# Where step 1 counts its put-off rows on TensorE: at the end of an iteration, pinned in program order

## The chip, the cores and the metric

The kernel runs on one core of one Trainium2 chip. The metric is the device time of one execution in microseconds (us), lower is better; a time is the median of several executions. Engines are named as in the profile: PE is TensorE's matmul side and PEld its weight loads, DVE is VectorE, ACT is ScalarE, POOL is GpSimd, SP is SyncE, which here only issues DMAs.

## What is computed

Four graph layers over 4096 nodes with 256 features, each followed by a residual and a layer norm. Layers 0, 2 and 3 are products of a 0/1 adjacency matrix with the features. Layer 1 is the one that matters here; it runs two steps (n = 0 and n = 1) of

```
logits = q @ k.T                 # 4096 x 4096, q and k from the current Xa
probs  = softmax(logits)
A      = for each row, keep the largest probs until their sum reaches 0.9, renormalize
Xf     = R @ Xf                  # R: the adjacency matrix + I, its rows scaled to sum 1
Xa     = A @ Xa
Z      = Z + Xf @ U1[n].T + Xa @ U2[n].T
```

The kernel never sorts a row of 4096. It finds the threshold of each row from the largest values of 18 groups of columns (step 1), and a row for which that is not sure is put off: it is marked bad, its number goes into a list in HBM, and the listed rows are computed later, 128 at a time, by a slower way that always works.

## The kernel before, in words

Rows are worked on in tiles of 128. In step 1, `run_step(1, ...)` (L944) has an iteration for each tile i from -2 to 31, in which three tiles are in flight:

- tile i+2 (`nxt`): its logits are made, in eight chunks of 512 columns (g = 0 to 7, NLC = 8), by PE (`logits_chunk`, L415) and copied out by ACT (L416).
- tile i+1 (`cd`): DVE takes the group maxima (`peak_groups`, L434, 18 instructions, and L466, L467), ACT the exponentials (L457), DVE the largest 72 candidates (`tops`, L529 and L533), the threshold and the mark bad (`pick`, L551 to L566). Then `flag` (L584) counts the bad rows, and `settle` (L643) zeroes what lies under the threshold: one pass over the row for ties (L660) and four passes over quarters of it (L665).
- tile i (`st`): PE transposes its kept probabilities (`turn`, L746, copied out by ACT, L749) and multiplies them with Xa (L769). One iteration later `mix` (L816) turns the result (L186, ACT L188), multiplies it with U1 and U2 (L822), and DVE adds the residual (L824) and does two layer norms, each with one power on POOL (L200).

From tile 11 on, an iteration also makes one row tile of the product with R (`neighbours`: ACT L685, PE L688, ending in L690). Three times (after i = 9, 20 and during i = 31) 128 put-off rows are taken from the list (`take_rows`, L883) and become a job, whose stages (`put_off`, L897; five probes of L499, then candidates and settling) run beside the ordinary tiles.

`pieces` (L725) writes the iteration as a loop over g; after the work of chunk g it runs the functions that `run_step` has put down for g with `at(g, f)`. So `at(4, flag, cd)` (L1018) traces the flag after the logits, the product and the neighbours of chunk 4.

What `flag` issues for a tile: two matmuls of one column, L594 (sum of `bad` over the tile, on all partitions) and L595 (bad rows before each row), into one half of the PSUM bank `mm_bank`; three small DVE instructions that turn them into places in the list (`sofar` L597, `slot` L601, `slots` L602); and one indirect DMA from POOL that writes the row numbers into `list_d` (L608). `query` (L395) and `mix` (L822) use the same bank. `take_rows` loads 128 entries of the list (L888, on SP's queue), clamps them (`from_l`, L890, DVE) and gathers their rows (L812, POOL).

The order in which each engine gets its instructions is not the traced order. The framework plans it: it simulates the engines with durations of its own, and gives an engine, among the instructions whose inputs are ready in that simulation, the one traced first. On the chip each engine then follows this fixed order, and an instruction whose input is late holds up all that stand behind it on its engine. `tc.keep_in_program_order(ins)` adds an edge of order (no semaphore, no instruction) from the instruction traced just before on the same engine to `ins`: the planner may place `ins` only behind that one. It doesn't keep later traced instructions from being placed ahead of `ins`.

Of the kernel before, what the change touches and what calls it, by code (L numbers as in the profile page):

```python
# [57 lines left out]
def gnn_stack(ctx, tc, x, adjt, adjn, w0, b0, w1, w2t, w3t, u1t, u2t, ln_g, ln_b, w2, b2, w3, b3, out):  # L58
# [3 lines left out]
    nc = tc.nc  # L62
# [3 lines left out]
    NLC = N // LC  # L66
# [20 lines left out]
    def half(bank):  # L87
        turns[bank] ^= 1
        return (mm_bank if bank == "mm" else acc_bank)[:, turns[bank], :]
# [90 lines left out]
    def transposed(*srcs):  # L180

        n = 2 * len(srcs)
        ps = ps_tr.tile([P, 4, P], F32, tag="tr", name="tr")
        for s, src in enumerate(srcs):
            for c in range(2):
                nc.tensor.transpose(ps[:, 2 * s + c, :], src[:, c * P : (c + 1) * P], ident)  # L186
        t = work.tile([P, 4, P], F32, tag="xt", name="xt")
        nc.scalar.copy(t[:, :n, :], ps[:, :n, :])  # L188
        return t
# [168 lines left out]
    with tc.tile_pool(name="l1", bufs=1, reuse_waits="tile") as l1:  # L358

        cur = {"late": False, "n": 0, "nef_done": False}  # L360
# [4 lines left out]
        ones_sq = l1.tile([P, P], F32, name="ones_sq")  # L365
# [23 lines left out]
        def query(xi, xt=None):  # L389

            if xt is None:
                xt = transposed(xi)
            ps = half("mm")
            for c in range(2):
                nc.tensor.matmul(ps[:, :P], wq_sb[:, c, :], xt[:, c, :], start=(c == 0), stop=(c == 1))  # L395
            up = upper(ps[:, :P])
            q = [work.tile([P, P], F32R, tag=f"q{k}", name=f"q{k}", bufs=3) for k in range(2)]
            nc.scalar.copy(q[0], up)
            nc.vector.tensor_sub(q[1], ps[:, :P], up)
            return q  # L400
# [17 lines left out]
        def logits_in(l):  # L418

            nc.vector.memset(l[:, N:], -1.0)  # L420
            return l

        def small(tag, w=1, dt=F32, bufs=2):
            if cur["late"]:
                return cur["lw"].tile([P, w], dt, tag=tag, name=f"{tag}_l", bufs=2 if w == 1 else 1)
            return work.tile([P, w], dt, tag=tag, name=tag, bufs=bufs)
# [157 lines left out]
        def flag(st):  # L584


            pb = half("mm")
            later = st.get("later")
            if later is None:
                nc.tensor.matmul(pb[:1, 0:1], st["bad"], ones_col, start=True, stop=True)  # L590
                st["nb"] = small("nbad", 1, I32)[:1, :]
                nc.scalar.copy(st["nb"], pb[:1, :1])
                return
            nc.tensor.matmul(pb[:, 0:1], ones_sq, st["bad"], start=True, stop=True)  # L594
            nc.tensor.matmul(pb[:, 1:2], before, st["bad"], start=True, stop=True)  # L595
            sofar, slot = small("sofar"), small("slot")
            nc.vector.tensor_add(sofar, later["base"], pb[:, 0:1])  # L597

            i = st["tile"]
            at, rows_i = slots_of[cur["n"]][:, i : i + 1], ids[:, i : i + 1]  # L600
            nc.vector.scalar_tensor_tensor(slot, pb[:, 1:2], later["base"], spare, op0=ALU.add, op1=ALU.subtract)  # L601
            nc.vector.scalar_tensor_tensor(at, slot, st["bad"], spare, op0=ALU.mult, op1=ALU.add)  # L602
            later["base"] = sofar
            if i == NT - 1 and cur["n"] == 0:

                st["to"] = to = small("to_last", 1, I32, 1)
                nc.vector.scalar_tensor_tensor(to, st["bad"], float(P), rows_i, op0=ALU.mult, op1=ALU.add)
            nc.gpsimd.indirect_dma_start(  # L608
                out=list_d[cur["n"]], out_offset=bass.IndirectOffsetOnAxis(ap=at, axis=0), in_=rows_i, in_offset=None)
# [314 lines left out]
        def left_over(n, e, later):  # L924

            count = work.tile([P, 1], I32, tag="count_l", name="count_l", bufs=1)
            nc.vector.tensor_scalar(count, later["base"], float(P - 1 - LATER[n] * P), 0.0, op0=ALU.add, op1=ALU.max)
            nc.vector.tensor_scalar(count, count, P.bit_length() - 1, None, op0=ALU.arith_shift_right)
            v = nc.values_load(count[0:1, 0:1], min_val=0, max_val=NT - LATER[n])
            with tc.For_i(0, v, 1) as k:  # L930
                cur["late"] = True
                st, xg = take_rows(n, bass.ds(k * P + LATER[n] * P, P), e)
                all_logits(st, query(xg))
                peak(st)
                exp_rows(st)
                st["t"], st["left"], st["base"] = small("t_thr"), small("left"), None
                for _ in settle(st, True):
                    pass
                pieces(n, st, None, {})
                for f in after(n, st):  # L940
                    f()
                cur["late"] = False

        def run_step(n, es):  # L944
# [37 lines left out]
            for i in range(-2, NT):  # L982
                st = tiles.pop(i, None)
                cd = tiles.get(i + 1)
                nxt = None
                if i + 2 < NT:

                    nxt = {"tile": i + 2, "q": cur["qs"].pop(0), "e": logits_in(es[i % 2]), "later": later, "G": {}}
                    tiles[i + 2] = nxt
                if i + 1 == NT and n == 0:  # L990
                    for fs in last:
                        for f in fs:
                            f()
                    last = []
                    left_over(n, es[NT % 2], later)
                ops = {}

                def at(g, f, *args):
                    ops.setdefault(g, []).append(lambda: f(*args))

                for g, fs in zip((1, 2), last):
                    for f in fs:
                        at(g, f)
                if 0 < i + 2 < NT - 1:
                    turned = []
                    g = 1 if n else 6
                    at(g - 1, lambda i, turned: turned.append(transposed(cur["xa"][:, i + 3, :])), i, turned)
                    at(g, lambda turned: cur["qs"].append(query(None, turned[0])), turned)
                if cd is not None:
                    peak_groups(cd, NG_LATER if n else ngr)  # L1010
                    at(1, exp_rows, cd)
                for job in jobs:
                    at(1, advance, job)
                if cd is not None:
                    rounds = ROUNDS if n else ROUNDS_FEW
                    at(2, tops, cd, rounds)
                    at(2, pick, cd, rounds)
                    at(4, flag, cd)  # L1018
                    if n == 0:
                        for k in range(8):  # L1020
                            at(4 + k // 2, gather, cd, k)
                    else:
                        at(5, lambda cd: [None for _ in settle(cd)], cd)
                if n == 0 and st is not None:
                    for k in range(8, KEPT):
                        at(k // 2 - 4, gather, st, k)
                for job in jobs:
                    if n and i + 1 == NT:
                        at(4, advance, job)
                    at(6, advance, job)  # L1030
                if i + 1 == NT and n == 0:
                    cur["next"] = load_halves(es[1 - NT % 2], xf_d, nc.sync)
                if i < 0:
                    now = FIRST[n][i + 2]
                else:
                    now = [i + 2] if FIRST[n][1][-1] < i + 2 < NT else []
                pieces(n, st, nxt, ops, now)
                last = [[f] for f in after(n, st)] if st is not None else []
                if i in starts:
                    k = starts[i]  # L1040
                    if len(jobs) > (i == NT - 2):
                        last = finish(jobs.pop(0), last)
                    e = es[NT % 2] if k + 1 == LATER[n] else es[2]
                    jobs.append({"stages": put_off(n, k, e, later)})
                    if i < NT - 2:
                        advance(jobs[-1])
# [185 lines left out]
```

## Time and profile before

| what | us |
|---|---|
| median of 3 runs (3055.0 to 3058.85) | 3057.41 |
| the profiled execution | 3159.93 |
| its span, first to last instruction | 3158.2 |
| what lies around the span | 1.7 |
| mean granted TensorE clock | 0.971 |
| PE busy in the span | 2895.0 (92%) |
| DVE busy | 2247.3 (71%) |
| ACT busy | 1723.6 (55%) |
| POOL busy | 678.1 (21%) |
| first and last flag of step 1 on PE (from the span's start) | 1387.43 and 2439.92 |

The profiled execution is longer than the median of the other runs; all times of instructions are from it and are set against its own 3159.93 us. In a list of waits a line says which engine and line waited for which, then the sum in us, how often, and the longest. In a timeline the columns are the start in us from the span's start, the duration in us, and the instruction; x4 means four merged into one row, and a bracket at the end is the idle time of the engine just before it and what ended that.

### The profile page before, as it was taken

The page shows a single profiled execution, that of the slowest core. Times are in us where ns is not written, and L with a number is a line of the kernel's source. Part 1 is how long each engine was busy: PE and PEld are TensorE (multiplying, and loading weights), DVE is VectorE, ACT ScalarE, POOL GpSimd, SP SyncE. Part 2 cuts the span into 40 slices and gives each one's busy share as a digit, 9 for nine tenths or more (in the row PEclk, how much of TensorE's full clock was granted, in tenths as well). Part 3 has the DMA queues.
Part 4 walks back from the last instruction along what each step waited for, and adds up shares of the span by engine and source line. Part 5 has one row for each costly group of instructions (what it writes and reads, how often), then busy time and mean ns, then how long its engine had stood idle before and what let it go on. Part 6 is the DMA issues. An engine that isn't in the chain of part 4 may idle for free. (4 is left out here: it accounts for less than half of the span.)

```text
span 3158.2 us, 44761 instructions
## 1 busy us (share of the span) xinstructions
PE 2895.0 (92%) x14052; PEld 2271.4 (72%) x14052; DVE 2247.3 (71%) x7159; ACT 1723.6 (55%) x2883; POOL 678.1 (21%) x812
## 2 busy tenths in 40 slices
PE   7999888999999997789998999999999987999998
PEld 3788656777777775567777777878877645777886
DVE  4666667888888876267998999967999644444444
ACT  3555545566666654465554655546555425666664
POOL 1121245555555554000000000010000110000000
PEclk9999989999999998899999999999999998999999
DMA  9996455777777774240000111011110324333332
GB/s 172 158 178 126 77 100 110 122 131 132 128 130 136 132 133 132 79 110 17 26 23 26 30 35 38 29 36 32 34 38 24 104 92 158 108 108 95 107 109 77
DMA packets 242873, 286.82 MB, mean 91 GB/s; under 512 B 32928, under 2 KB 199776, under 8 KB 242624
## 3 DMA queue, kind: packets, MB, share of 16 engines
q0 software_dynamic: 41728, 91.69, 22.1%
q1 hardware_dynamic: 188656, 180.93, 18.6%
q10 hardware_dynamic: 12240, 11.23, 1.1%
q8 instruction: 114, 1.87, 0.2%
q14 instruction: 135, 1.11, 0.2%
HBM read 318.06 MB, written 66.32 MB: 122 GB/s over the span
## 5 line engine op out<-in xcount | busy, mean ns | idle before, releaser
L688 PE MATMUL acc_r<-xh,adjq 128*128 128x512 f32 x2048 | 625.9, 434 | 33.2 <-ACT adjq L685 17.5
L769 PE MATMUL acc_bank<-xa,at 128*128 128x256 f32 x2240 | 551.0, 386 | 26.2 <-ACT at L749 25.8
L685 ACT CAST adjq<-adj 128x512 fp32r<-128x512 fp8e4 x512 | 315.5, 619 | 371.0 <-PE acc_r L688 214.6
L688 PEld LDWEIGHTS acc_r<-xh,adjq 128*128 128x128 f32 x2048 | 382.8, 193 | 132.0 <-ACT adjq L685 37.7
L674 POOL DMA_INDIRECT G<-x_d,cols x416 | 403.5, 970 | 326.0 <-PE acc_bank L763 172.2
L769 PEld LDWEIGHTS acc_bank<-xa,at 128*128 128x128 f32 x2240 | 409.9, 193 | 85.9 <-ACT at L749 37.5
L416 ACT COPY e<-lg 128x512 f32<-128x512 f32 x544 | 315.1, 586 | 231.2 <-PE lg L415 159.9
L434 DVE MAX8 cand<-e 128x8 f32<-128x228 f32 (+1 forms) x1088 | 385.0, 399 | 34.4 <-ACT e L416 31.7
L415 PE MATMUL lg<-kS,q 128*128 128x512 f32 x1088 | 391.6, 442 | 6.0 <-issue 3.8
L200 POOL TENSOR_TENSOR rstd<-ve,mhalf 128x1 f32<-128x1 f32 x166 | 100.3, 604 | 1331.8 <-DVE ve L198 1246.3
L1112 ACT CAST a<-a 128x1024 fp32r<-128x1024 fp8e4 x256 | 268.3, 1049 | 165.4 <-PE acc L176 127.1
L531 DVE FIND_INDEX8 cols<-top,e 128x8 uint32<-128x4096 f32 x64 | 282.8, 4419 | 0.0
L176 PE MATMUL acc<-xh,a 128*128 128x512 f32 x1024 | 260.1, 407 | 21.2 <-DMA a<-adj_d 16.1
L176 PE MATMUL acc<-y0h,a 128*128 128x512 f32 x1024 | 249.9, 397 | 0.0
L176 PEld LDWEIGHTS acc<-xh,a 128*128 128x128 f32 x1024 | 191.7, 190 | 67.8 <-ACT xh L152 23.5
L176 PE MATMUL acc<-yh,a 128*128 128x512 f32 x1024 | 237.9, 394 | 0.0
L763 PE MATMUL acc_bank<-G,dg 128*128 128x256 f32 x832 | 228.1, 392 | 8.3 <-DVE dg L761 4.1
L176 PEld LDWEIGHTS acc<-yh,a 128*128 128x128 f32 x1024 | 192.2, 188 | 43.8
L176 PEld LDWEIGHTS acc<-y0h,a 128*128 128x128 f32 x1024 | 187.9, 188 | 39.0 <-issue 0.6
L749 ACT COPY at<-at_ps 128x512 f32<-128x512 f32 x288 | 168.7, 588 | 84.7 <-PE at_ps L746 83.0
L415 PEld LDWEIGHTS lg<-kS,q 128*128 128x128 f32 x1088 | 183.4, 193 | 29.6 <-ACT e L416 9.2
L763 PEld LDWEIGHTS acc_bank<-G,dg 128*128 128x128 f32 x832 | 156.3, 195 | 38.6 <-DVE dg L761 4.5
(287 smaller groups left out, 4414.1 us busy)
## 6 DMA issues: line engine op xcount, KB each, us to landing
adj<-adj_d SPq DMA_DIRECT2D x256, 128.0 KB
a<-adj_d SPq DMA_DIRECT2D x256, 128.0 KB
a<-in_adjt POOLq DMA_DIRECT2D x64, 256.0 KB
adj_d<-a SPq DMA_DIRECT2D x64, 256.0 KB
adjn<-in_adjn POOLq DMA_DIRECT2D x64, 256.0 KB
x_d<-x SPq DMA_DIRECT2D x64, 128.0 KB
xf_d<-xf_new SPq DMA_DIRECT2D x64, 128.0 KB
xf<-xf_d SPq DMA_DIRECT2D x64, 128.0 KB
```

What stands on the lines that cost most here:

```text
L176: nc.tensor.matmul(acc, a[:, j, :], halves(jt), start=(jt == 0), stop=(jt == NT - 1))
L415: nc.tensor.matmul(pl[:, :LC], q[k], kS[:, s], start=(k == 0), stop=(k == 1))
L416: nc.scalar.copy(l[:, s], pl[:, :LC])
L434: nc.vector.max(dst[:, 8 * g : 8 * g + 8], src[:, g * w : min((g + 1) * w, N)])
L531: nc.vector.max_index(st["at"][:, 8 * r : 8 * r + 8], t8, st["e"][:, :N])
L674: nc.gpsimd.indirect_dma_start(out=g, out_offset=None, in_=x1_d, in_offset=bass.IndirectOffsetOnAxis(ap=st["at"][:, k : k + 1], axis=0))
L685: nc.scalar.copy(a, cur["a8"][:, g % 2 * GP : (g % 2 + 1) * GP, :])
L688: nc.tensor.matmul(acc_r, a[:, j, :], xf[:, jt, :], start=(jt == 0), stop=False)
L749: nc.scalar.copy(at[:, :G, :], ps[:, :G, :])
L763: nc.tensor.matmul(acc_a, dg[:, k % 4, :], st["G"][k], start=(k == 0), stop=(k == KEPT - 1))
L769: nc.tensor.matmul(acc_a, ats[g][:, j, :], cur["xa"][:, jt, :], start=(jt == 0), stop=(jt == NT - 1))
L1112: nc.scalar.copy(a, a8)
```

## The change

In step 1 the flag is traced after the last chunk of the iteration (NLC - 1 is 7), and its first matmul is pinned behind what was traced before it on PE: the last matmul of the product (L769), or of the row tile of R (L690) where there is one. Step 0 keeps chunk 4 and gets no pin. Nothing is added to or taken from what the engines compute.

```
-            nc.tensor.matmul(pb[:, 0:1], ones_sq, st["bad"], start=True, stop=True)
+            total = nc.tensor.matmul(pb[:, 0:1], ones_sq, st["bad"], start=True, stop=True)
+            if cur["n"]:
+                tc.keep_in_program_order(total)
             nc.tensor.matmul(pb[:, 1:2], before, st["bad"], start=True, stop=True)
...
-                    at(4, flag, cd)
+                    at(NLC - 1 if n else 4, flag, cd)
```

## The prediction

> **What bounds the kernel now.** Only step 1's tiles are touched, 1387 to 2447 us, so I asked for the waits by stretch, not for the page's shares. First the sums of three stretches (length, then busy time of PE, PEld, DVE, ACT, POOL, the granted clock, DMA share, GB/s): 1445 to 1692 holds eight flags and no put-off job; the other two hold the jobs.
>
> ```profile
> 1445.00:1692.00 247.00, 228.29 (x1203) 191.60 (x1202) 226.23 (x780) 126.33 (x212) 18.70 (x25) 1.00 0.08 24
> 1735.00:2060.00 325.00, 309.83 (x1557) 254.95 (x1556) 300.22 (x1029) 184.86 (x306) 20.68 (x27) 0.99 0.13 33
> 2160.00:2440.00 280.00, 267.71 (x1357) 221.37 (x1355) 267.40 (x924) 153.81 (x258) 18.44 (x25) 1.00 0.14 33
> ```
>
> PE and DVE are both busy for 92 to 96%: each bounds the other, and a wait taken from one helps only as far as the other isn't late next. The waits of PE and then of DVE between 1735 and 2450 us:
>
> ```profile
> PE mm_bank L594 <- DVE bad L566: 15.8, 15, 1.7
> ...
> DVE h L824 <- PE mm_bank L822: 15.7, 9, 6.6
> ...
> DVE sofar L597 <- PE mm_bank L595: 4.2, 11, 1.8
> ```
>
> PE's largest wait is the flag's: 15.8 us at 15 of the 20 flags there, about 1.05 each. Between 1445 and 1692 the flag waits for nothing; PE waits are these:
>
> ```profile
> PE acc_bank L769 <- ACT at L749: 10.4, 8, 1.4
> PE mm_bank L395 <- DVE h L824: 8.3, 9, 1.0
> ```
>
> **Flags with a put-off job beside them.** PE's timeline at one of them, then DVE's:
>
> ```profile
> 1837.68 0.38 PE L594 MATMUL mm_bank<-bad,ones_sq 128*128 128x1 f32 x2 [1.32 <-DVE bad L566]
> ...
> 1841.66 3.75 PE L688 MATMUL acc_r<-xh,adjq 128*128 128x512 f32 x15
> 1845.26 1.03 PE L746 MATMUL at_ps<-ident,e 128*128 128x128 f32 x8
> ```
>
> ```profile
> 1843.60 1.27 DVE L665 SCALAR_TENSOR_TENSOR e<-e,t_thr 128x1024 f32<-128x1024 f32 x1
> ```
>
> The flag stops PE for 1.32 us. But the same tile's transposes (L746, 1845.26) need the first quarter of settle, done at 1843.60 + 1.27 = 1844.87: PE arrives 0.39 us after that. Without the flag's wait it would come 1.32 earlier and wait 0.93 there. So of each wait only the smaller of it and this slack comes back. For the 15 flags, in order: 0.16, 0.22, 0.38, 0.69, 0.32, 0.16, 0.26, 0.28, 0.41, 0.24, 0.41, 1.69, 0.26, 0.16, 1.19: 6.8 of 15.8 us; 9.0 move to L746. And an earlier PE shortens the run only where DVE waits for PE. In these iterations DVE's waits for h (L824) are 0.55, 6.61, 0.51, 0.33 and 3.25 us, and PE has 0.38, 0.69, 0.32, 0.41 and 0.26 to give them: 0.38 + 0.69 + 0.32 + 0.33 + 0.26 = 2.0. DVE's waits at sofar for the flag's matmuls go too, since the flag then stands where DVE finished bad long ago and reads it later: 4.2 less the one of 1.8 that lies outside the jobs, 2.4. Sum: **-4.4 us**.
>
> **Flags without a job** (nine, 1458 to 1693, 29.3 us apart). PE's timeline:
>
> ```profile
> 1632.40 1.89 PE L769 MATMUL acc_bank<-xa,at 128*128 128x256 f32 x8
> 1634.13 0.28 PE L594 MATMUL mm_bank<-bad,ones_sq 128*128 128x1 f32 x2
> 1634.27 0.36 PE L595 MATMUL mm_bank<-bad,before 128*128 128x1 f32 x2
> 1634.50 0.71 PE L415 MATMUL lg<-kS,q 128*128 128x512 f32 x2
> ...
> 1647.23 1.13 PE L769 MATMUL acc_bank<-xa,at 128*128 128x256 f32 x4 [1.12 <-ACT at L749]
> ```
>
> From the start of the eight L769 to the next L415 it is 2.10 us with the flag, 1.54 one chunk later without (1638.11 to 1639.65): a flag takes 0.56 us of PE. It lies between L395 and the last logits (1639.65), on the path: last logits, ACT copy, maxima, candidates, settle's tie pass (4.43), h, L395, logits again; PE's only idle time in it, 0.9 us, is at L395, ahead of the flag. At the end of the iteration (1642.03) the flag stands ahead of L746, L415 and L688, and behind those PE idles 1.1 to 1.4 us until ACT has done the exponentials: there it is free. That is 9 x 0.56 = 5.0. DVE can follow: it waits 0.57 us for the last logits, and POOL's list write (1.02 us, now just before the second L200 of a tile, where DVE waits 9.1/8 = 1.14 us against 9.9/21 = 0.47 with jobs) moves out of its way. The Trainium skill speaks against this sum: TensorE: Matmul & The Clock Gate, "Back-to-back issue gap", gives a matmul of 1 to 64 columns an issue floor of about 25 ns, so four (each of the pair runs as two) would be 0.1 us and the move worth 0.9 in all. The row has each with a weight load of its own (0.19) and 0.56 in sum; I take the row. **-5.0 us**, between 0 and -5.0.
>
> **The other flags**: 1387 and 1429 (the start) and 2041 to 2135 wait for nothing and PE is full there: 0.
>
> **What the move delays.** The three DVE instructions (0.13 + 0.21 + 0.22) only move. `mm_bank` is held from the flag until DVE has read it; next to want it is L822, 10.5 us after an iteration's end here (1642.2 to 1652.7), 12 in the row of 1837. A DVE instruction in the way lasts 4.4 at most, so 0; without that cover, up to 4.4 per tile. POOL: behind the list write wait L200 and the jobs' gathers; it takes 1.02 us and POOL is busy 7%: 0. SP: only the list's load waits for it, with the adjacency and row loads behind. The pin is an edge without a wait: 0.
>
> The list itself is needed at once three times. POOL's and SP's timelines at the first:
>
> ```profile
> 1694.36 1.02 POOL L608 DMA_INDIRECT list_d<-ids,slots  x1 [3.46 <-DVE kept L580]
> ```
>
> ```profile
> 1702.72 0.33 SPq L888 DMA_DIRECT2D to_l<-list_d  x1
> ```
>
> From the write's issue to the load 8.4 us pass, and then DVE stands still at L890: 5.58, 5.20 and 7.23 us (18.0 in sum). The Trainium skill's page DMA: Bandwidth & Descriptors ("Anatomy of one DMA — SWDGE (gpsimd) path") has a fixed cost of about 2.0 us for such a write: by it the list would be in HBM before DVE asks, and a later flag would cost nothing. The rows say 8.4, so each us of delay can be a us of DVE. The delays, from the flag to the last matmul that it is pinned behind: 1692.70 to 1700.6 = 7.9; 2074.71 to 2085.7 = 11.0; 2439.92 to 2446.4, of which DVE's tie pass (to 2444.5) and L205 already take all but 0.5. Bounds: if the planner moves L890 by as much, the wait stays as long and the price is 0.5; if L890 keeps its place, 7.9 + 11.0 + 0.5 = 19.4. I take 0.5, since L890 depends on the flag in the planner's simulation too; the 5 us of today are what that simulation has too little for a DMA, the same wherever it stands. The last job has cover besides: its settling ends its first quarter at 2552.5, and PE, at the zu matmuls (L871), comes to it at 2566.9.
>
> **Sum**: -4.4 - 5.0 + 0.5 = -8.9 us. The profiled execution would go from 3159.9 to 3151.0. The median of the runs shown is 3.2% lower; I take the difference over as it is: **3048.5**.
>
> **Rivals.**
> 1. Likeliest, as above: 3048.5, own range 3042 to 3055. Chance 0.45.
> 2. The wait only changes place. DVE is the bound with jobs, all 15.8 us come back at L746, and without jobs the planner fills the freed slot so that the flag's 0.56 is on the path again. For: the 9.0 us found above, DVE at 95%. Against: the idle time behind L688. 0, or 3057; that the planner lets later traced work pass the pinned flag, so that it stands in the next iteration and changes nothing, ends here too. Chance 0.22.
> 3. All of PE's wait is gain, since the planner moves L688 of R ahead of L746 and so hides the rest: -15.8 - 5.0 = 20.8, 3036.6. For: 15 L688 stand there in the row above. Against: DVE's idle time in these stretches is mostly not PE's doing. Chance 0.12.
> 4. Slower: the put-off rows come late. L890 stays where it is in DVE's order, and DVE, strictly in order, stands for 19.4 us more, with SP's loads behind L888: +19.4 - 8.9 = +10.5, 3067.9. It decides as soon as the list lands more than 8.9 us later, summed over the three loads, than L890's place in DVE's order moves. For: the 8.4 us of a list write, and DVE's 18.0 us there now. Against: the planner knows the dependence. Chance 0.21.
>
> Faster or slower by 0.2% is 6.1 us, about what a measurement of this kernel can tell from no change. Of rival 1, 0.35 lies beyond that and 0.10 within: faster 0.35 + 0.12 = 0.47, same 0.22 + 0.10 = 0.32, slower 0.21. The range reaches down to rival 3 and up to rival 4: 3037 to 3067.
>
> **What would show it.** Right: no wait of L594 for bad; L746 waits for L665, about 9 us in sum, in the iterations with a job; the nine iterations without one 28.7 us apart instead of 29.3, with the flag between L769 and L746 and less than 1.4 us idle at L769 behind L688; L205 there waiting about 0.5. L890 waiting 18 us in sum again. Wrong: L890 waiting over 27 us (rival 4), L822 or L395 waiting for slot (the bank), iterations still 29.3 us apart (rival 2), or a planner's order changed in more places than the flag's, which no step here prices.

## The result and the profile after

The changed kernel takes 3052.85 us (median of 19 runs, 3045.61 to 3062.08), the kernel before 3058.85 (19 runs beside it). The ratio is 0.9981, 95% interval 0.9973 to 0.9988: faster by 6.0 us, just short of the 6.1 us (0.2%) from which the prediction counts the kernel as faster. It had said 3048.5 and -8.9 us.

The profiled execution of the changed kernel takes 3051.51 us, that of before 3159.93. Nearly all of this difference lies in step 0, which the change doesn't touch: up to the first mark of step 1 (the end of DVE's L566 for tile 0) before needs 1374 us and the changed kernel 1275. The experiments show that this is no effect of the change: the kernel before needs 1272 us in another execution, and on one chip, where its median was 3157.66 us, every profiled kernel needs 1375 to 1377. So I compare from that mark on, with a second profiled execution of the kernel before (`before_again`, below). Lines of the changed kernel behind L596 have numbers that are higher by 2.

The same three stretches as before the change, the first two shifted by the 99 us, the third by 110:

```profile
1346.00:1593.00 247.00, 228.76 (x1209) 192.41 (x1208) 227.93 (x783) 127.36 (x214) 18.64 (x25) 1.00 0.09 24
1636.00:1961.00 325.00, 310.50 (x1568) 256.36 (x1568) 302.51 (x1043) 186.56 (x308) 21.17 (x28) 0.99 0.15 33
2050.00:2330.00 280.00, 268.66 (x1372) 223.90 (x1372) 269.54 (x935) 156.67 (x258) 18.47 (x25) 1.00 0.17 34
```

PE and DVE are busier by less than one per cent: DVE 227.93 us of 247 where it was 226.23. The waits of PE and DVE between 1636 and 2345 us say what became of the flag's wait:

```profile
PE at_ps L748 <- DVE e L667: 9.6, 10, 1.4
...
DVE h L826 <- PE mm_bank L824: 8.7, 5, 3.1
...
DVE m L466 <- DVEq L652: 4.2, 1, 4.2
...
PE mm_bank L594 <- DVE bad L566: 1.6, 2, 1.4
...
DVE sofar L599 <- PE mm_bank L597: 1.1, 4, 0.6
```

PE's wait at the flag falls from 15.8 to 1.6 us, and 9.6 of it stand at the transposes now, as forecast (9.0). DVE's wait for h falls from 15.7 to 8.7. Other waits of PE grow, for h at L395 from 1.4 to 5.5 us and for xt at L824 from 1.1 to 3.3, so that all of PE's waits in this stretch fall only from 32.1 to 28.5. The third line is new: DVE stands for 4.2 us at the register branch of a put-off job (L652).

At a flag without a job, PE's timeline is what the change meant it to be:

```profile
1483.70 0.81 PE L771 MATMUL acc_bank<-xa,at 128*128 128x256 f32 x3
1484.35 0.28 PE L594 MATMUL mm_bank<-bad,ones_sq 128*128 128x1 f32 x2
1484.49 0.36 PE L597 MATMUL mm_bank<-bad,before 128*128 128x1 f32 x2
1484.71 0.63 PE L748 MATMUL at_ps<-ident,e 128*128 128x128 f32 x4
...
1489.65 1.99 PE L771 MATMUL acc_bank<-xa,at 128*128 128x256 f32 x8 [1.07 <-ACT at L751]
```

Where the 6.0 us come from (us from mark to mark, the mark being the end of L566 of a tile; "end" is the end of the span):

| tiles | before_again | after | difference |
|---|---|---|---|
| 0 to 1 | 31.74 | 32.85 | +1.1 |
| 1 to 10, no job | 275.45 | 274.18 | -1.3 |
| 10 to 12, first list load | 81.89 | 81.45 | -0.4 |
| 12 to 20, first job | 273.20 | 273.33 | +0.1 |
| 20 to 23, second load | 133.17 | 128.69 | -4.5 |
| 23 to 31, second job | 266.98 | 262.93 | -4.1 |
| 31 to the end, third load | 718.25 | 721.26 | +3.0 |
| sum | 1780.7 | 1774.7 | -6.0 |

The first profile of before and `before_again` differ by up to 2.0 us in one such row. Set against the first profile the sum is -9.4, so it is luck that it is -6.0 here, as between the medians. The row beside the first job is the least steady: with the flags of tiles 11 to 20 moved it was 272.8 to 280.7 us long in after and four of the kernels below (all_but_load2, after_take_later, job_tiles and nopin, which has the longest and differs from after by the pin alone), and 272.5 to 275.7 in six profiles with these flags at their old place. The eight periods of 2 to 10 are far steadier: 234.0 us in both profiles of before, 233.0 after. The largest gain sits where the prediction had none, at the second load.

### The profile page after: what moved, and what is told of

Read it like the earlier page. It is cut to its first block, busy times and chain, and to the rows that moved or that the text cites. A ratio compares the mean times of both kernels' runs of the same rounds, so it can differ in the third digit from the quotient of the medians.

```text
span 3049.8 us, 44765 instructions
## 1 busy us (share of the span) xinstructions
PE 2850.4 (93%) x14052; PEld 2256.0 (74%) x14052; DVE 2246.1 (74%) x7159; ACT 1730.8 (57%) x2883; POOL 679.7 (22%) x812
## 5 line engine op out<-in xcount | busy, mean ns | idle before, releaser
L690 PE MATMUL acc_r<-xh,adjq 128*128 128x512 f32 x2048 | 617.7, 429 | 18.7 <-issue 8.6
L771 PE MATMUL acc_bank<-xa,at 128*128 128x256 f32 x2240 | 540.3, 381 | 16.8 <-ACT at L751 16.6
L690 PEld LDWEIGHTS acc_r<-xh,adjq 128*128 128x128 f32 x2048 | 380.8, 191 | 109.1 <-ACT adjq L687 26.2
L415 PE MATMUL lg<-kS,q 128*128 128x512 f32 x1088 | 391.4, 441 | 0.3 <-ACT e L416 0.2
L415 PEld LDWEIGHTS lg<-kS,q 128*128 128x128 f32 x1088 | 182.7, 192 | 23.7 <-ACT e L416 8.0
L748 PE MATMUL at_ps<-ident,e 128*128 128x128 f32 x1152 | 175.9, 275 | 17.9 <-DVE e L667 17.8
```

Source lines behind the costliest of these rows:

```text
L415: nc.tensor.matmul(pl[:, :LC], q[k], kS[:, s], start=(k == 0), stop=(k == 1))
L690: nc.tensor.matmul(acc_r, a[:, j, :], xf[:, jt, :], start=(jt == 0), stop=False)
L748: nc.tensor.transpose(ps[:, j, :], e[:, (g * G + j) * P : (g * G + j + 1) * P], ident)
L771: nc.tensor.matmul(acc_a, ats[g][:, j, :], cur["xa"][:, jt, :], start=(jt == 0), stop=(jt == NT - 1))
```

## The experiments

The runs were made in four groups, each on one chip, with medians of the kernel before of 3060.30, 3072.18, 3157.66 and 3070.53 us; ratios are within a group.

**before_again**: the kernel before, unchanged.

> The kernel before once more, for a second profile. In the first one step 0, which the change doesn't touch, took 816.5 us from the first tile's mark bad (L566) to the last, in the profile after 720.1; the rest of the program differs by some 10 us. If the 96 us belong to that one execution, step 0 takes about 720 here and the profiled time is about 3059; if they belong to the kernel before, it takes 816 again. In both cases the stretches of step 1 should repeat within 0.5 us: tiles 1 to 10 in 275.5, 10 to 12 in 82.9, 12 to 20 in 273.7, 20 to 23 in 135.2, 23 to 31 in 265.6, and 719.6 from the last mark to the end.

Measured: 3054.36 us, 1780.7 from the mark to the end (1784.1 in the first profile). The 96 us belong to step 0 of the first profile. Not all stretches repeat within the 0.5 us that was expected: tiles 20 to 23 took 133.2 and not 135.2.

**early_tiles**, **load2_only** and **all_but_load2** make the change for some flags alone: for tiles 0 to 9 (`i < 9`, as below), for tile 21, whose flag the second load needs (`i == 20`), and for all but tile 21 (`i != 20`).

```
-            if cur["n"]:
+            if st.get("late"):
                 tc.keep_in_program_order(total)
...
-                    at(NLC - 1 if n else 4, flag, cd)
+                    cd["late"] = n == 1 and i < 9
+                    at(NLC - 1 if cd["late"] else 4, flag, cd)
```

> Only the flags of step 1's tiles 0 to 9 stand at the end of the iteration and are pinned; the other 22 stay after chunk 4. The theory of the prediction (the flag's 0.56 us of PE leave the path nine times): -5.0 us, periods of 28.7. The theory read from the trace after (the flag's three DVE instructions now stand among the candidates, L529, on the path, and give back 0.42 of the 0.56): -1.3 us, periods of 29.15, DVE waiting 1.1 for the last logits. Rival, only the change as a whole pays: 0.

> Only one flag is moved and pinned, that of tile 21, whose list write the second load of put-off rows waits for. The theory of the prediction: 0 to +0.5 us, the later list costs nothing and gains nothing. The theory read from the trace after (DVE's 5.2 us at from_l move behind the start of the job's product, so that PE works on instead of idling 4.0 us and then running at half speed for 2): about -6 us, all of it between the marks of tiles 20 and 23. Rival, the prediction's slower case: +8 to +11 there.

> All flags of step 1 moved and pinned but that of tile 21. The theory of the prediction: -8.9 as a whole, the same time as the kernel after. The theory read from the trace after: the 6.5 us between tiles 20 and 23 are gone, so -3 against the kernel before; PE idles 4.0 us at L771 and runs at half speed after it again.

Measured: early_tiles 0.9999 (0.9990 to 1.0007), its period 29.14 us instead of 29.29. load2_only 0.9990 (0.9983 to 0.9997), tiles 20 to 23 in 129.35 us. all_but_load2 0.9995 (0.9985 to 1.0005), tiles 20 to 23 in 134.07. One flag of 32 brings about half of the gain. The ten early ones bring nothing that the whole time shows (-3.1 to +2.1 us, which leaves out the -5.0 of the prediction), though their period did fall by 0.15.

What that flag does is seen on PE. First before, then after the change, with the sums of 12 us behind it:

```profile
2087.93 0.61 PE L415 MATMUL lg<-kS,q 128*128 128x512 f32 x2
2092.55 3.78 PE L769 MATMUL acc_bank<-xa,at 128*128 128x256 f32 x8 [4.00 <-ACT at L749]
```

```profile
2092.00:2104.00 12.00, 11.46 (x45) 9.51 (x46) 9.96 (x30) 4.02 (x9) 2.40 (x3) 0.72 0.15 45
```

```profile
1986.64 0.63 PE L415 MATMUL lg<-kS,q 128*128 128x512 f32 x2
1988.46 1.99 PE L771 MATMUL acc_bank<-xa,at 128*128 128x256 f32 x8 [1.19 <-ACT at L751]
```

```profile
1988.00:2000.00 12.00, 11.54 (x63) 10.11 (x64) 6.41 (x29) 4.82 (x10) 1.96 (x2) 1.00 0.16 44
```

Before, PE idles 4.00 us and then does eight L769 in 3.78 us instead of 1.99; the granted clock is 0.72 over these 12 us. After, it idles 1.19 us and keeps the full clock. DVE's own wait for the list is as long as ever:

```profile
2086.01 0.15 DVE L890 TENSOR_SCALAR from_l<-to_l 128x1 int32<-128x1 int32 x1 [5.20 <-DMA to_l<-list_d]
```

```profile
1995.30 0.15 DVE L892 TENSOR_SCALAR from_l<-to_l 128x1 int32<-128x1 int32 x1 [5.29 <-DMA to_l<-list_d]
```

But it stands elsewhere in DVE's order. Before, it comes ahead of the row maximum m (L466, at 2087.09) and of the tile's candidate rounds (the L529 after it start at 2087.41). ACT's exponentials (L457) wait for m, the copies that PE needs (L749) stand behind them on ACT, and so PE waits at last. After, it comes behind m and the rounds (the last L529 is at 1989.70), while PE has a product to do. ACT before and after:

```profile
2087.86 3.71 ACT L457 ACTIVATE e<-e,m 128x4096 f32<-128x4096 f32 x1 [2.68 <-DVE m L467]
```

```profile
1983.77 3.71 ACT L457 ACTIVATE e<-e,m 128x4096 f32<-128x4096 f32 x1 [0.29 <-DVE m L467]
```

Without tile 21's flag PE idles 3.79 us and the eight take 3.78 again (all_but_load2); with it alone, 1.19.

**behind_logits** pins the flag behind the last logits of the iteration (L415 of chunk 7):

```
                     logits_chunk(nxt["e"], nxt["q"], g)
+                if g == NLC - 1:
+                    for f in ops.get("last", ()):
+                        f()
...
-                    at(NLC - 1 if n else 4, flag, cd)
+                    at("last" if n else 4, flag, cd)
```

**nopin** is the changed kernel without the two lines of the pin. **take_later** is the kernel before with the second job's first stage taken within the next iteration and not at the end of this one:

```
-                    if i < NT - 2:
+                    if i < NT - 2 and not (n and k == 1):
                         advance(jobs[-1])
```

**job_tiles** makes the change for tiles 11 to 20 and 22 to 30 alone (`i > 9 and i not in (20, 30)`).

> The flags of step 1 are traced and pinned behind the last logits (L415) of the iteration instead of behind the last of the product, 1.7 us earlier on PE, so that DVE can do the three instructions while it waits 1.2 us for the last logits, before the candidates. The theory read from the trace after (the three on DVE give back 0.42 of 0.56 us in tiles 1 to 10): periods of 28.7 there instead of 29.15, -5.0 us in these tiles, 3.7 below the kernel after. Rival, that something else than the three holds these tiles (the exponentials, L395): periods stay at 29.15.

> The flag is traced after chunk 7 and not pinned. If the pin decides: the planner puts the flag back to where the mark is ready in its simulation, PE waits for the mark as before (about 15 us at L594), and the time is the kernel before's, 0. If the place in the traced order is enough: the same as after, -6.

> The kernel before with all flags where they were; only the second load of put-off rows is taken some 10 us later, from within the next iteration (after chunk 1) instead of at the end of tile 20's. The theory read from the trace after (what pays at tile 21 is where DVE's wait for the list falls, not the flag): PE doesn't idle 4.0 us there, the granted clock stays at 1.00, and 4 to 7 us go between tiles 20 and 23, less if the job's last stage slips behind the end of the tiles. The theory of the prediction: 0.

> Only the flags of tiles 11 to 20 and 22 to 30 are moved and pinned, those with a job beside them; tiles 0 to 10, 21 and 31 stay. The theory of the prediction: -4.4 us, with PE's wait at L594 gone and 9 us at the transposes (L748) in its place. From the trace after: -0.3 between tiles 12 and 20, -2.6 between 23 and 31, -3 in sum. Rival, DVE alone bounds these tiles: 0.

Measured: behind_logits 1.0002 (0.9992 to 1.0012): the early period is 28.95 us, the shortest of all, but PE waits for bad again (4.0 us with the jobs) and tiles 20 to 23 take 132.0. nopin 0.9976 (0.9968 to 0.9983), PE's wait at the flag 1.6 us: the traced place does all of it, the pin nothing that can be measured. take_later 0.9967 (0.9954 to 0.9980): 10 us, although PE's idle time at the load stays, at 4.48 us, against what I expected: L890 stands ahead of m in DVE's order there too. Tiles 20 to 31 take 391.4 instead of 400.2; why a half iteration's shift of the job's stages helps so much stays open. job_tiles 1.0012 (1.0003 to 1.0021): slower by 3.7 us (0.9 to 6.5), though all but 1.6 us of PE's wait at the flag is gone from these tiles. Something in them takes the gain back.

**dve_double** issues the three DVE instructions behind the flag twice; **after_take_later** is the change with take_later's edit; **late_tiles** makes the change for tiles 21 to 30 (`i > 19 and i != 30`). The edit of dve_double:

```
+            if cur["n"]:
+                nc.vector.tensor_add(sofar, later["base"], pb[:, 0:1])
+                nc.vector.scalar_tensor_tensor(slot, pb[:, 1:2], later["base"], spare, op0=ALU.add, op1=ALU.subtract)
+                nc.vector.scalar_tensor_tensor(at, slot, st["bad"], spare, op0=ALU.mult, op1=ALU.add)
```

> The changed kernel with the three small DVE instructions behind the flag (sofar, slot, slots; 0.13 + 0.21 + 0.22 us) issued twice at the same place. Theory A (moved to the iteration's end they lie in the candidates' serial chain of the next tile and give back most of what the flag's matmuls had left the path by): the early tiles' period goes from 29.14 to 29.4-29.7 us, tiles 2 to 10 from 232.97 to 235.5-237.5, and step 1 as a whole is 4 to 12 us longer than with the change. Theory B (they only moved, and lie in DVE's slack, as the prediction said): the period stays within 0.05 of 29.14 and the whole within 2 us of the changed kernel.

> The changed kernel with the second put-off job's first stage taken within the next iteration and not at the end of this one. If the two edits' gains are separate (the change: 6.0 us; the later stage alone: about 10 us) the sum is 14 to 16 us, a ratio of about 0.995. If both live on the same place (the second list load and the iterations behind it) the gain is that of the better one, 8 to 11 us, ratio about 0.9968, and tiles 20 to 31 take about 391 us as with the later stage alone; with separate gains they take about 383.

> The change for the flags of tiles 21 to 30 alone (the second list load and the iterations behind it), all other flags where they were. If the change's gain is all there, this gives 7 to 9 us (4.5 at the load, 4.1 behind it), ratio 0.997 to 0.9977, and the tail is not longer than before since the last flag stays. If the earlier flags carry gain too, as the prediction had it (5.0 in tiles 1 to 10, 2 to 3 in tiles 11 to 20), it gives no more than 3 us.

Measured: dve_double 0.9993 (0.9981 to 1.0006), early period 29.12 us: its theory A had said 29.4 to 29.7, and by the period it fell and theory B (29.14) held. The pieces of the period say more; DVE's in a tile without a job (tile 7 to 8), us from start to start, with the changed kernel's line numbers:

| from L566 to | before | after | dve_double | behind_logits |
|---|---|---|---|---|
| h (L826) | 5.15 | 5.07 | 5.07 | 5.07 |
| the second norm's L205 | 9.60 | 8.55 | 8.56 | 8.56 |
| m (L466) | 4.69 | 5.28 | 5.06 | 5.45 |
| the first L533 | 0.65 | 1.03 | 1.23 | 0.65 |
| the next L566 | 9.21 | 9.20 | 9.20 | 9.21 |
| period | 29.29 | 29.14 | 29.13 | 28.95 |

In `after` m comes 0.54 us earlier, which fits the 0.56 of PE that the flag no longer takes from the logits. Then 0.38 go again between m and the first L533:

```profile
1484.46 0.30 DVE L466 TENSOR_REDUCE m<-cand 128x1 f32<-128x144 f32 x1
1484.68 0.17 DVE L524 TENSOR_REDUCE top<-cand 128x1 f32<-128x18 f32 x1
1484.89 0.16 DVE L599 TENSOR_TENSOR sofar<-sofar,mm_bank 128x1 f32<-128x1 f32 x1
1484.96 0.21 DVE L603 SCALAR_TENSOR_TENSOR slot<-mm_bank,sofar,spare 128x1 f32<-128x1 f32 x1
1485.09 0.14 DVE L467 TENSOR_SCALAR m<-m 128x1 f32<-128x1 f32 x1
1485.15 0.30 DVE L529 MAX8 top<-cand 128x8 f32<-128x144 f32 x1
1485.37 0.20 DVE L604 SCALAR_TENSOR_TENSOR slots<-slot,bad,spare 128x1 int32<-128x1 f32 x1
```

The flag's DVE work now stands among the rounds L529 and L533, each of which needs the one before it, and where nothing else covers it. Doubling it adds 0.20 there (not 0.38: part falls into the gaps of the rounds), but the planner also puts one transpose ahead of L395 on PE, m comes 0.22 earlier, and the period doesn't show it. In behind_logits the same three stand ahead of m, in DVE's wait for the last logits, cost 0.17, and the gain stays: 0.34. So the place of these three decides: behind_logits shows it by the period, dve_double by the one piece alone.

after_take_later 0.9957 (0.9941 to 0.9972): tiles 20 to 31 take 386.0 us, 5.4 less than with take_later alone, nearer to what separate gains would give (383) than to one shared gain (391). late_tiles 0.9982 (0.9972 to 0.9993), the same as the whole change. The flags of tiles 0 to 20 and 31 earn nothing together that these ratios show. The parts don't add up: early_tiles -0.3, job_tiles +3.7 and load2_only -3.1 us make +0.3, and the whole change -6.0. Each is good to 2 or 3 us; what is left between them stays open.

**best**. In tiles 12 to 20 there is the new wait at L652. DVE's and POOL's timelines in `after`:

```profile
1814.32 4.22 DVE L434 MAX8 cand<-e 128x8 f32<-128x228 f32 x14
1822.78 0.30 DVE L466 TENSOR_REDUCE m<-cand 128x1 f32<-128x144 f32 x1 [4.23 <-DVEq L652]
```

```profile
1814.58 1.01 POOL L610 DMA_INDIRECT list_d<-ids,slots  x1 [18.46 <-DVE slots L604]
```

The first job's branch (it skips the slow repair, as always here) is taken at 1815.40, and DVE's sequencer comes to the next instruction at 1822.67, 7.27 us later; the MAX8 that were queued before the branch last only until 1818.54. PE stands for 3.2 us behind this (L395, for h), and then the granted clock is 0.50 from 1824.6 to 1827.9. POOL's list write of tile 16 leaves 0.82 us ahead of this branch. All runs side by side:

| runs | list write ahead of the branch | branch to next instruction | DVE's wait |
|---|---|---|---|
| before, before_again, early_tiles, load2_only, late_tiles, take_later (tile 16's flag at its old place) | 11.13 | 3.18 | 0.1 |
| after, all_but_load2, nopin, after_take_later | 0.82 | 7.27 to 8.14 | 4.2 to 5.1 |
| job_tiles | 1.19 | 7.60 | 4.9 |
| behind_logits | 1.62 | 6.65 | 3.6 |
| dve_double | 3.72 | 0.57 | 0.6 |

dve_double doesn't fit a rule of the distance alone. Nor does the branch of the second job. There the moved list write leaves 0.45 us ahead in after, all_but_load2, behind_logits, nopin, job_tiles and late_tiles, and the next instruction comes 3.17 us behind the branch, with no wait. In `after` this branch is at 2215.58, and L466 has no bracket:

```profile
2215.13 1.03 POOL L610 DMA_INDIRECT list_d<-ids,slots  x1 [19.48 <-DVE slots L604]
```

```profile
2214.76 3.95 DVE L434 MAX8 cand<-e 128x8 f32<-128x228 f32 x13
2218.86 0.30 DVE L466 TENSOR_REDUCE m<-cand 128x1 f32<-128x144 f32 x1
```

For the list write speaks when the wait ends: in all six runs that have it the next instruction comes 8.1 to 9.0 us behind the write's issue, and the three list loads, which wait for such a write, leave 6.5 to 9.3 us behind it. The trace has a DMA packet of code (8192 bytes) that starts 1.0 us behind the branch in both before and after; the Trainium skill, Runtime: NRT & Kernel Launch, "Instruction fetch mechanics", says that a taken branch to a page that isn't at hand makes the engine wait for such a fetch; no run here shows where the target's page was. The test leaves tile 16's flag where it was, on top of after_take_later:

```
-            if cur["n"]:
+            if st.get("late"):
                 tc.keep_in_program_order(total)
...
+                    cd["late"] = n == 1 and i != 15
+                    at(NLC - 1 if cd["late"] else 4, flag, cd)
```

> The change with the later first stage of the second put-off job, and with one flag left at its old place: that of tile 16, whose list write otherwise leaves 0.8 to 1.6 us ahead of the branch of the first put-off job. Theory A (in the kernels with this flag moved, the branch's code fetch stands behind the list write's DMA, so that DVE gets its next instruction 6.7 to 8.1 us after the branch and stands for 3.6 to 5.1 us): the next instruction comes 3.2 us or less after the branch, DVE's wait at m (L466) falls from 4.3 to 1.5 us or less, tiles 16 to 17 take 48 to 50 us and not 53.2, and the ratio is 0.9945 +- 0.001. Theory B (the branch is late for another reason, such as where its code lies): 6.7 us or more after the branch again, m waits 3.5 us or more, and the ratio stays at 0.9957 or worse.

```profile
1821.01 3.94 DVE L434 MAX8 cand<-e 128x8 f32<-128x228 f32 x13
1825.09 0.30 DVE L466 TENSOR_REDUCE m<-cand 128x1 f32<-128x144 f32 x1
```

```profile
1810.57 1.01 POOL L610 DMA_INDIRECT list_d<-ids,slots  x1 [8.19 <-DVE slots L604]
```

Measured: the wait is gone (no bracket at L466), the next instruction comes 3.18 us behind the branch at 1821.80, tiles 16 to 17 take 49.99 us instead of the 53.17 of after_take_later, tiles 12 to 20 273.2 instead of 277.6 (though `after` took 273.3 with the wait). The ratio is 0.9935 (0.9919 to 0.9951), 18 us between the medians of these runs (3070.53 to 3052.43), better than the changed kernel's 0.9981 by intervals that don't meet. But take_later's gain is in it, and the interval of after_take_later (0.9941 to 0.9972) does meet this one, so what tile 16's flag alone is worth in the whole time isn't shown. What is shown is that the wait comes with this flag's new place and goes with it (after_take_later against best). That its list write does it, as theory A said, fits the time at which the wait ends; but at the second job's branch a write as close ahead is not enough, and what else it takes stays open. How a write of 4-byte rows would hold up the fetch isn't shown either: the code's packet itself moves at the same time in both.

## Why the prediction was right or wrong

The direction and the range held. The size came out at two thirds, by other places than the prediction's steps, so that its nearness is in good part luck.

**Flags with a job beside them, -4.4.** The waits moved as forecast: 9.6 us went to the transposes (9.0 forecast), 1.6 stayed, and DVE's waits for h and sofar fell by 7.0 and 3.1 (2.0 and 2.4 forecast; the stretch also holds the second load). The gain did not come: these flags alone cost 3.7 us (job_tiles). In the tiles of the second job the period falls by 0.34 to 0.48 us in each of four iterations (23 to 27), to 0.01 us the same in late_tiles and job_tiles, 1.6 in all. Of the other 2.5 of that row, 1.7 is one iteration (27 to 28), which in before_again alone took 49.2 us and in before, early_tiles and load2_only 47.6; the rest isn't settled. In those of the first job the sum is +0.1, with 4.2 us of new wait at L652 in it, and up to 7.4 us more in the other executions with these flags moved. The step that failed is "POOL: [...] 0" and with it the branch that the prediction didn't look for: the list write was priced as 1.02 us of a free engine, while moving tile 16's flag brought DVE a wait of 3.6 to 5.1 us at the first job's branch (that the write brings it is likely, not shown).

**Flags without a job, -5.0.** The 0.56 us of a flag did leave the path, in the row's size and not in that of the issue floor: 0.54 in m. L205 waits 0.36 us (0.5 forecast), and PE idles 1.07 behind L690. The term that failed is "The three DVE instructions [...] only move", which was priced at 0. They move into the candidates' rounds and give back 0.38 of it each time; the period fell by 0.15 and not by 0.56, the nine together by 1.3.

**The other flags, 0, and the pin, 0.** Tiles 0 to 1 got 1.1 us longer in the changed kernel's profile (0.3 in early_tiles, nothing in nopin, both of which move that flag), which stays open. The pin is shown to do nothing for the time (nopin).

**The list loads, +0.5.** The planner did move L890 with the flag, so rival 4 (10.5 us slower) didn't come: L892 waits 5.37, 5.29 and 9.28 us, 19.9 in sum (18 forecast). At the third load the moved flag costs more than 0.5: from tile 31's mark to L892 it takes 21.9 to 22.4 us in after, all_but_load2, behind_logits and nopin, and 19.9 to 20.9 with tile 31's flag unmoved (both profiles of before, early_tiles, load2_only, job_tiles, late_tiles), some 1.5. The rest of the +3.0 in that row is not the flag's: from L892 to the end, where nothing is changed, the executions spread from 695 to 704 us.
The step had looked at how long the wait is, and not at who stands behind it. At the second load that was the whole matter: the wait is as long, but it stands behind m and the candidate rounds, PE has work meanwhile, and 4.5 us come back. Of these 2.3 are idle time (3.49 us in before_again, 1.19 after) and 1.5 the clock that is no longer cut (eight L769 in 3.46 us, then in 1.99). The clause that failed here is "the same wherever it stands".

**Rivals.** Rival 2 (the wait only changes place) describes tiles 0 to 20 well, for another reason than DVE being the bound; rival 3 didn't come, 9.6 us did move to L748. The -8.9 was near -6.0 because a gain not seen (second load, -4.5) stood against two losses not seen (0.38 each on nine flags, 4.2 at the branch): that is luck.

## What to carry to other kernels

When a step moves, follow each of its instructions to the place where it lands, the small ones on the other engines and its DMA too: here 0.5 us of DVE work fell into a serial chain, and behind one moved flag DVE stood 4 us at a branch. A wait of an in-order engine is priced by what stands behind it there: the same 5 us or so cost 4.5 less once they came behind the work that PE was waiting for. Try a moved step for one group of tiles at a time: one flag of 32 carried half the gain, and leaving another one out took a wait of 4 us away again.

## What the runs showed of the hardware

- At the second list load PE idled 3.49 to 4.48 us and then did the next eight L769 in 3.40 to 3.78 us (before, before_again, all_but_load2, take_later); after 1.19 us it did them in 1.99. The 4.00 us of before so cost 1.8 us more than themselves. The Trainium skill, TensorE: Matmul & The Clock Gate, "HAM oscillation — how this bites in real kernels", puts the bound at about 3.4 us of idle time. These four fit it (3.49 and more against 1.19), but the length of the idle time doesn't decide alone here: the same eight matmuls took 3.68 us after 2.12 us of idle time in load2_only (granted clock 0.50), 1.99 after 2.37 in after, and 2.00 after 3.30 in behind_logits (granted clock 1.00 in both):

```profile
1869.56 3.68 PE L771 MATMUL acc_bank<-xa,at 128*128 128x256 f32 x8 [2.12 <-ACT at L751]
```

```profile
1866.33 1.99 PE L771 MATMUL acc_bank<-xa,at 128*128 128x256 f32 x8 [2.37 <-ACT at L751]
```

- The taken branch of the first job held DVE's sequencer for 3.2 us at most where tile 16's flag stood at its old place. With the flag moved it held it for 6.65 to 8.14 us in six kernels, an indirect write of 128 rows of 4 bytes having left 0.8 to 1.6 us ahead, and for 0.57 in dve_double, where the write left 3.7 us ahead. At the second job's branch it was 3.17 at most with a write 0.45 us ahead. The MAX8 queued before the branch cover 3.1 us of each but dve_double's.
- On one chip step 0 took about 1375 us to the first mark of step 1 (as in the first profile of before), and on the others 1272 to 1292; its program is the same in all, and the cause is open. The mean period of tiles 2 to 10 with their flags unmoved was the same to 0.01 us, 29.25 to 29.26.
